# Gate and up products in column halves, their moving operand laid out in DRAM during the attention stage

## The chip, the core and the metric

The kernel runs on one core of a Trainium2 chip. The metric is the device time of one execution in microseconds, as a median over several runs. The core's engines each work through their own instructions in order: TensorE (PE; its weight loads are listed apart as PEld), VectorE (DVE), ScalarE (ACT), GpSimd (POOL) and SyncE (SP). In this kernel SP issues every DMA.

## What is computed

A block of one layer on x of shape (4, 512, 512), all in float32: a layer norm, then attention and a gated feed-forward network side by side, both added to x. The weights of the feed-forward network are not given; they are Catmull-Rom splines through control points.

```python
def spline_reconstruct(control_points, out_size, in_size):
    n = out_size * in_size
    idx, f = _catmull_rom_grid(control_points.shape[0], n)
    p0, p1, p2, p3 = (control_points[idx[0]], ..., control_points[idx[3]])
    w = 0.5 * (2.0 * p1 + (p2 - p0) * f + (2.0 * p0 - 5.0 * p1 + 4.0 * p2 - p3) * f2
               + (3.0 * p1 - p0 - 3.0 * p2 + p3) * f3)
    return w.reshape(out_size, in_size)
...
gate_w = spline_reconstruct(gate_cp, 2048, 512)
up_w = spline_reconstruct(up_cp, 2048, 512)
down_w = spline_reconstruct(down_cp, 512, 2048)
gate = jnp.einsum('bsh,ih->bsi', hidden_states, gate_w)
up = jnp.einsum('bsh,ih->bsi', hidden_states, up_w)
inter = jax.nn.silu(gate) * up
return jnp.einsum('bsi,hi->bsh', inter, down_w)
...
xn = _layernorm(x, axis=-1)
x = x + attention(xn, Wq, bq, Wk, bk, Wv, bv, Wo, bo) + ffn(xn, gate_cp, up_cp, down_cp)
```

A row of gate_w or up_w is a cubic between knots that lie some 129 samples apart. So the kernel doesn't multiply by whole rows of 512 entries. For each of 16 tiles of 128 rows it keeps 64 numbers per token: 44 single samples of xn near the knots (4 windows of 11), and 20 moments, sums of xn against cubics over the stretches between the windows. The product of a tile has a contraction of 64 in place of 512.

## The kernel before

The program has two stages. The **attention stage** covers all four batches: layer norm, projections, scores, softmax, values, and the output projection. It is a loop over 64 units (batch, group of four heads, tile of 128 queries). `items[n]` lists what is added at unit n: a projection, a transpose, a load. In this stage the gate, up and down weights are also built from their control points, by DVE (L600 to L684). `feat[0]`, a tile that stays for the whole program, serves as space for the tables of this work until item 52.

Two things per batch go to DRAM in this stage: the normed x, transposed (`keep_samples`, L491, to `samples[b]`; at items 0, 12, 28 and 44) and the moments (`stretch_moments`, L498, to `moments[b]`; at items 20, 18, 34 and 60). `load_feat` (L525) brings them back as the moving operand `feat[b]`, [128, 2 parts, 4, 512]. Its 128 partitions are four strips of 32 rows, one for each tile of a group of four; a strip holds 22 samples and 10 moments in each part. It issues 24 transfers for a batch, 16 of samples with 11 rows (88 KB) and 8 of moments with 10 rows (80 KB). For batch 0 they stand at item 52; for the others in the second stage.

The **feed-forward stage** follows five written plans (L1201). Plan b does the gate and up products of batch b, and works off the down products of batch b - 1 in between:

- G and U (`gate`, L1075, and `up`, L1080; V is U with other PSUM banks): `product` (L1057) for a group q of four tiles. For each of two parts, each of the four strips is multiplied by its 128 weight columns into its own PSUM bank: 8 matmuls with 32 rows and 128 columns, 512 wide. ACT takes gate's four banks (silu, L1078), DVE multiplies up's four banks by the result (L1085), GpSimd copies it (L1086), and SP moves odd rows between banks (L1090, `inner<-made`) and single rows to `lone` (L1095, L1099).
- m and M (`inner_moments`, L1101): moments of the inner activations, matmuls of 32 rows and 64 columns. The last step is followed by copies and sums on DVE and ACT (T, `add_moments`, L1135).
- R (`down_values`, L1152): the down product from single inner values, matmuls of 32 rows and 64 columns.
- S (`down_moments`, L1172): its part from the moments, 128 rows and 64 columns, then on DVE the addition of attention's result (`res`, loaded by L, L1148) and the store.
- P (`proj`, L466): the rest of batch 3's output projection, 128 rows and 128 columns.
- F: `load_feat` of batch b + 1, in two pieces: F0 with three of the four windows, F1 with the last.

PSUM has two sets of four banks here, `ps_g` for G and U, `ps_o` for V, m, R and P. Every float32 matmul shows as two records in the trace.

The order on each engine is the order of the program (`in_order`, L379, pins it), SP included: an issue that waits holds up all the issues behind it.

Of the kernel before, what the change touches and what calls it, by code (L numbers as in the profile page):

```python
# [12 lines left out]
F32 = mybir.dt.float32  # L13
# [5 lines left out]
P = 128  # L19
B, S, D, H = 4, 512, 512, 16  # L20
# [3 lines left out]
NB = D // P  # L24
# [19 lines left out]
Q32 = 32  # L44
ND = 64
NE = 8
NCV = 5
NX = 9 + 4
NW, NW4 = 11, 4
NST = NW4 + 1  # L50

# [153 lines left out]
def window(g, w):  # L205

    return 8 * g + 129 * w - 1
# [187 lines left out]
def block_kernel(  # L395
# [17 lines left out]
    nc = tc.nc  # L413
    xpf = xp.rearrange("b s d -> (b s) d")

    keep = ctx.enter_context(tc.tile_pool(name="keep", bufs=1))
    dram = ctx.enter_context(tc.tile_pool(name="dram", bufs=1, space=bass.MemoryType.DRAM))
# [7 lines left out]
    samples = [dram.tile([D + P + Q32, S], F32, name=f"samples{b}") for b in range(B)]  # L425
    moments = [dram.tile([NRT * 4 * NST, S], F32, name=f"moments{b}") for b in range(B)]

    feat = {0: keep.tile([P, 2, NB, S], F32, name="feat")}


    wT = keep.tile([P, NB, 4, P], F32, name="wT")
# [90 lines left out]
                if at == k:  # L522
                    nc.sync.dma_start(out=rows[s], in_=o[half * 64 : (half + 1) * 64])

    def load_feat(b, windows=range(NW4)):  # L525

        strip = lambda j: feat[b][j * Q32 : (j + 1) * Q32]
        turns = [(0, 2, 1, 3), (1, 3, 0, 2)]
        for w in windows:
            for j in turns[w % 2]:  # L530
                rows = samples[b][window(j, w) + 1 :][:P].rearrange("(q r) d -> r q d", q=NB)
                nc.sync.dma_start(
                    out=strip(j)[w % 2 * NW : (w % 2 + 1) * NW, w // 2], in_=rows[:NW]
                )
            if w % 2:
                rows = moments[b].rearrange("(q r) d -> r q d", q=NB)
                for j in turns[0]:
                    at = (2 * j + w // 2) * 2 * NST
                    nc.sync.dma_start(
                        out=strip(j)[2 * NW :, w // 2], in_=rows[at : at + 2 * NST]  # L540
                    )


    with ExitStack() as att:
# [19 lines left out]
        for k in range(2):  # L564
# [24 lines left out]
            out=dist[:, S - P :],  # L589
# [10 lines left out]
        def row_weight_steps():  # L600
            size = NB * 2 * P
            shaped = lambda a: a.rearrange("p (q x n) -> p q x n", q=NB, x=2)
            spare = [
                feat[0].rearrange("p h c s -> p (h c s)")[:, k * size : (k + 1) * size]
                for k in range(4)
            ]
            temps = [wd[:, :size], wd[:, size : 2 * size]]
            tabs, points = {}, {}

            def load(c):  # L610
                def go():
                    tabs[c], points[c] = (shaped(a) for a in spare[c % 2 * 2 :][:2])
                    nc.sync.dma_start(out=tabs[c], in_=coef[c])
                    for k in range(NB):
                        strip = slice(k * Q32, (k + 1) * Q32)
                        nc.sync.dma_start(
                            out=spare[c % 2 * 2 + 1][strip],
                            in_=rowpts[c, k].partition_broadcast(Q32),
                        )

                return go

            def term(c, w):
                to = wT[:, :, 2 * w : 2 * w + 2, :]
                tmp = shaped(temps[w]) if c else to

                def times():
                    own = points[c].rearrange("p (w q) x n -> p w (q x) n", w=2)[:, w]
                    own = own.unsqueeze(2).to_broadcast([P, NB, 2, P])
                    nc.vector.tensor_tensor(tmp, tabs[c], own, ALU.mult)  # L630

                def plus():
                    nc.vector.tensor_tensor(to, to, tmp, ALU.add)

                return [times, plus] if c else [times]

            steps = [(0.0, load(0)), (0.0, load(1))]
            for c in range(NCG):
                for w in range(2):
                    steps += [(1.2, half) for half in term(c, w)]  # L640
                if c + 2 < NCG:
                    steps.append((0.0, load(c + 2)))
            return steps


        def down_steps():
            size = 5 * P
            spare = feat[0].rearrange("p h c s -> p (h c s)")
            given, at = [], 0
            for _, lo, hi, _ in DOWN_STEPS:  # L650
                given.append((at, (hi - lo) * P))
                at += P * (hi - lo) * P

            def load(n):
                def go():
                    at, width = given[n]
                    for k, source in enumerate((downtab, downpts)):
                        to = spare[:, (n % 3 * 2 + k) * size :][:, :width]
                        part = source[at : at + P * width].rearrange("(p x) -> p x", p=P)
                        nc.sync.dma_start(out=to, in_=part)  # L660

                return go

            def term(n):
                kind, lo, hi, c = DOWN_STEPS[n]
                width = given[n][1]
                to = (dR if kind == "v" else dM)[:, lo:hi].rearrange("p a n -> p (a n)")
                tmp = wd[:, n % 2 * size :][:, :width] if c else to
                tab, own = (spare[:, (n % 3 * 2 + k) * size :][:, :width] for k in range(2))

                def times():
                    nc.vector.tensor_tensor(tmp, tab, own, ALU.mult)

                def plus():
                    nc.vector.tensor_tensor(to, to, tmp, ALU.add)

                return [times, plus] if c else [times]

            steps = [(0.0, load(n)) for n in range(3)]
            for n in range(len(DOWN_STEPS)):  # L680
                steps += [(0.9, half) for half in term(n)]
                if n + 3 < len(DOWN_STEPS):
                    steps.append((0.0, load(n + 3)))
            return steps  # L684
# [284 lines left out]
        for b in range(B):  # L969
            at = 4 * NHG * b  # L970
            items[max(at - 4, 0)].append(lambda b=b: keep_samples(b))
            items[(20, 18, 34, 60)[b]].append(lambda b=b: stretch_moments(b))
        items[52].append(lambda: load_feat(0))
        weights = deque(row_weight_steps() + down_steps())


# [79 lines left out]

    def product(b, q, w, pool, tag):  # L1057

        ps = [pool.tile([P, S], F32, name=tag) for _ in range(NB)]
        for part in range(2):  # L1060
            for k in range(NB):
                rows = slice(k * Q32, (k + 1) * Q32)
                nc.tensor.matmul(  # L1063
                    ps[k],
                    lhsT=wT[rows, q, 2 * w + part, :],
                    rhs=feat[b][rows, part, q, :],
                    start=(part == 0),
                    stop=(part == 1),
                )
        return ps  # L1070

    around, turning = {}, [False] * B
# [121 lines left out]
    for load, _ in last[:3]:  # L1194
# [4 lines left out]


    plans = [  # L1201
# [5 lines left out]
    ]  # L1207
# [1 line left out]
    def carry_out(b, steps):  # L1209
        for step in steps.split():  # L1210
            kind, which = step[0], step[1:]
            tiles = range(*map(int, which.split(":"))) if ":" in which else None
            if kind == "G":
                gate(b, int(which))
            elif kind == "U":
                up(b, int(which))
            elif kind == "V":
                up(b, int(which), ps_o, "o")
            elif kind == "P":
                last[int(which)][1]()  # L1220
                if int(which) == 0:
                    last[3][0]()
            elif kind == "M":
                inner_moments(b - 1, tiles, ps_g, "g")
            elif kind == "m":
                inner_moments(b - 1, tiles, ps_o, "o")
            elif kind == "F":
                if int(which) == 0:
                    feat[b + 1] = (keep if b % 2 else featp).tile([P, 2, NB, S], F32, name="feat")
                load_feat(b + 1, (range(NW4 - 1), [NW4 - 1])[int(which)])  # L1230
            elif kind == "T":
                add_moments(b - 1, 3)
            elif kind == "R":
                down_values(b - 1, tiles, ps_o, "o")
            elif kind == "L":
                load_res(b - 1)
            else:
                down_moments(b - 1)
# [50 lines left out]
```

## Time and profile before

| | |
|---|---|
| median of 3 runs | 573.04 us (571.2 to 573.11) |
| the profiled execution | 576.39 us |
| its span, first to last instruction | 574.6 us |
| granted TensorE clock, mean | 0.997 |
| first product (L1063) starts | 409.5 us |
| L1063 in `ps_g`, 32x128, 512 wide | 432 records |
| L1063 in `ps_o` | 80 records |
| L1110 (m, M), 32x64 | 512 records |
| L1164 (R), 32x64 | 576 records |
| `feat<-samples` | 64 transfers of 88 KB |
| `feat<-moments` | 32 transfers of 80 KB |
| DMA moved in all | 67.73 MB, 118 GB/s in the mean |

The page gives busy time, the chain of waits that ended last, and groups of instructions by line. The chain, listed in order of time, shows for each step its start, its length and how many records it merges: where one TensorE step follows another without a gap, TensorE set the pace; where a DMA or another engine stands between, that was waited for. The timeline of one engine lists its instructions with the idle time before them. Matmul ends are modelled, so the distance from the start of one step to the start of the next is read, not the busy time. Some matmul records are missing (of L1063's 512 all are there, in two groups).

### The profile page before, as it was taken

The page shows a single profiled execution, that of the slowest core. Times are in us where ns is not written, and L with a number is a line of the kernel's source. Part 1 is how long each engine was busy: PE and PEld are TensorE (multiplying, and loading weights), DVE is VectorE, ACT ScalarE, POOL GpSimd, SP SyncE. Part 2 cuts the span into 40 slices and gives each one's busy share as a digit, 9 for nine tenths or more (in the row PEclk, how much of TensorE's full clock was granted, in tenths as well). Part 3 has the DMA queues.
Part 4 walks back from the last instruction along what each step waited for, and adds up shares of the span by engine and source line. Part 5 has one row for each costly group of instructions (what it writes and reads, how often), then busy time and mean ns, then how long its engine had stood idle before and what let it go on. Part 6 is the DMA issues. An engine that isn't in the chain of part 4 may idle for free.

```text
span 574.6 us, 11201 instructions
## 1 busy us (share of the span) xinstructions
PE 563.5 (98%) x4012; PEld 277.7 (48%) x4012; DVE 355.6 (62%) x990; ACT 295.8 (51%) x782; POOL 184.2 (32%) x332
## 2 busy tenths in 40 slices
PE   7999999999999999999999999999999999999997
PEld 5645555544455555454555555555535334333343
DVE  5169998797587784637544444556243663854747
ACT  2266766565357556554755666677414521613413
POOL 2034534253134343222432442444133223122220
PEclk8999999999999999999999999999999999999999
DMA  8932246326443540212020004603557475685344
GB/s 297 336 83 75 73 116 189 110 50 201 129 156 111 187 164 0 66 38 74 2 88 6 1 2 103 118 6 79 131 134 184 95 191 187 114 196 199 114 150 161
DMA packets 34360, 67.73 MB, mean 118 GB/s; under 512 B 5664, under 2 KB 5664, under 8 KB 33792
## 3 DMA queue, kind: packets, MB, share of 16 engines
q1 hardware_dynamic: 34304, 67.01, 41.2%
q8 instruction: 32, 0.52, 0.4%
q14 instruction: 24, 0.20, 0.1%
HBM read 42.35 MB, written 15.29 MB: 100 GB/s over the span
## 4 chain that ended last, share of the span: by engine, by line
PE 84%; DVE 5%; DMA 5%; ACT 4%; SPq 1%; issue 1%; POOL 0%; DVEq 0%
PE mm L780 18%; PE mm L895 11%; PE mm L811 10%; PE g L1063 7%; PE mm L477 7%; PE s L838 7%; PE c L909 5%; PE o L1164 5%; PE o L1110 3%; PE o L477 3%; ACT p L867 2%; PE o L1181 2%; PE mm L505 2%; DMA inner<-made 2%; PE o L1063 2%; DVE p L851 1%
## 5 line engine op out<-in xcount | busy, mean ns | idle before, releaser
L882 POOL TENSOR_SCALAR p<-p,inv 128x128 f32<-128x128 f32 (+3 forms) x256 | 141.9, 573 | 258.7 <-DVE inv L880 247.1
L867 ACT ACTIVATE p<-p,low 128x128 f32<-128x128 f32 (+3 forms) x256 | 140.7, 552 | 46.3 <-DVE low L851 46.0
L851 DVE CUSTOM_DVE_ANT_0 p<-s,dist 128x128 f32<-128x128 f32 (+3 forms) x256 | 109.2, 482 | 36.7 <-PE s L838 35.7
L895 PEld LDWEIGHTS mm<-ident,p 128*128 128x128 f32 x640 | 71.0, 141 | 40.4 <-issue 25.5
L895 PE MATMUL mm<-ident,p 128*128 128x128 f32 x640 | 89.0, 278 | 1.2 <-ACT pT L900 0.7
L900 ACT COPY pT<-mm 128x512 f32<-128x512 f32 x96 | 55.2, 580 | 53.6 <-PE mm L895 53.3
L1086 POOL COPY made<-inner 128x512 f32<-128x512 f32 x64 | 39.0, 633 | 110.6 <-DVE inner L1085 85.2
L1078 ACT ACTIVATE act<-g 128x512 f32<-128x512 f32 x64 | 33.2, 603 | 63.9 <-PE g L1063 63.9
L811 PE MATMUL mm<-wv,xnT 128*128 128x512 f32 x128 | 59.8, 610 | 2.3 <-ACT xnT L765 2.3
L780 PE MATMUL mm<-xnT,wk 128*128 128x512 f32 (+1 forms) x136 | 59.3, 579 | 0.2 <-ACT xnT L765 0.2
L1063 PE MATMUL g<-feat,wT 32*128 32x512 f32 x432 | 58.6, 611 | 0.0
L780 PE MATMUL mm<-xnT,wq 128*128 128x512 f32 (+1 forms) x136 | 58.0, 569 | 0.3 <-ACT pT L900 0.2
L838 PE MATMUL s<-kT,qT 32*128 32x512 f32 (+3 forms) x512 | 51.1, 468 | 0.3
L898 DVE COPY pT<-mm 128x512 f32<-128x512 f32 x64 | 43.6, 687 | 9.1 <-PE mm L895 8.6
L867 ACT ACTIVATION_READ_ACCUMULATOR p<-p,low 128x1 f32 x256 | 48.4, 189 | 0.0
L1085 DVE TENSOR_TENSOR inner<-g,act 128x512 f32<-128x512 f32 x44 | 27.3, 684 | 31.7 <-issue 20.3
L477 PE MATMUL mm<-ctxT,wo 128*128 128x512 f32 x88 | 40.0, 597 | 0.0
L1063 PEld LDWEIGHTS g<-feat,wT 32*128 32x128 f32 x432 | 23.7, 184 | 32.2 <-issue 20.4
L909 PE MATMUL c<-pT,v 128*32 128x128 f32 (+3 forms) x512 | 37.8, 436 | 0.0
L780 PEld LDWEIGHTS mm<-xnT,wk 128*128 128x128 f32 x136 | 24.5, 189 | 25.3 <-issue 21.9
L811 PEld LDWEIGHTS mm<-wv,xnT 128*128 128x128 f32 x128 | 23.6, 194 | 26.8 <-issue 24.1
L780 PEld LDWEIGHTS mm<-xnT,wq 128*128 128x128 f32 x136 | 24.7, 190 | 23.2 <-issue 22.0
(100 smaller groups left out, 558.2 us busy)
## 6 DMA issues: line engine op xcount, KB each, us to landing
inner<-made SPq DMA_DIRECT2D x32, 256.0 KB
feat<-samples SPq DMA_DIRECT2D x64, 88.0 KB
xp<-in_xp_dram SPq DMA_DIRECT2D x16, 256.0 KB
samples<-xnT SPq DMA_DIRECT2D x4, 1024.0 KB
feat<-in_coef_dram SPq DMA_DIRECT2D x8, 512.0 KB
feat<-in_rowpts_dram SPq DMA_DIRECT2D x32, 128.0 KB
xt<-in_xT_dram SPq DMA_DIRECT2D x16, 256.0 KB
mid<-xt SPq DMA_DIRECT2D x16, 256.0 KB
```

The source lines that it names most:

```text
L477: nc.tensor.matmul(ps, lhsT=wsb["o"][:, c, r * P : (r + 1) * P], rhs=ctxT[b][:, c, :], start=(c == 0), stop=(c == NB - 1),)
L780: nc.tensor.matmul(ps[0][:, tokens], lhsT=wsb[name][:, c, hg * P : (hg + 1) * P], rhs=xnT[b][:, c, tokens], start=(c == 0), stop=(c == NB ...
L811: nc.tensor.matmul(ps[0], lhsT=xnT[b][:, c, t * P : (t + 1) * P], rhs=wsb["v"][:, c, :], start=(c == 0), stop=(c == NB - 1),)
L838: nc.tensor.matmul(banks[b, hg][j][:, at : at + (k + 1) * P], lhsT=qk[b, hg, "q"][rows, k * P : (k + 1) * P], rhs=qk[b, hg, "k"][rows, : ( ...
L851: nc.vector.tensor_tensor_reduce(out=p[:, j, :nk], in0=ps[j], in1=dist[:, S - nk :], scale=-SLOPES[hg * NG + j], scalar=BIG, op0=ALU.add, ...
L867: nc.scalar.activation(p[:, j, :nk], p[:, j, :nk], AF.Exp, bias=low[:, j : j + 1], scale=-1.0, accum_out=total[:, j : j + 1],)
L882: nc.gpsimd.tensor_scalar(p[:, j, :nk], p[:, j, :nk], inv[:, j : j + 1], 1.0, ALU.mult, ALU.mult)
L895: nc.tensor.transpose(ps[:, j, :], p[:, j, c * P : (c + 1) * P], ident)
L898: nc.vector.tensor_copy(out, ps)
L900: nc.scalar.copy(out, ps)
L909: nc.tensor.matmul(ps[j * HD : (j + 1) * HD, c * P :], lhsT=vals[b][:, c, hg * P + j * HD : hg * P + (j + 1) * HD], rhs=w[:, j, :], start= ...
L1063: nc.tensor.matmul(ps[k], lhsT=wT[rows, q, 2 * w + part, :], rhs=feat[b][rows, part, q, :], start=(part == 0), stop=(part == 1),)
```

## The change

`product` cuts the 128 columns of each matmul into two halves of 64, which go to the lower and upper 64 partitions of the same bank: 16 matmuls of 32x64 in place of 8 of 32x128. For each batch there is a new DRAM tensor `table[b]` in the layout of `feat`, which becomes [128, 4, 2, 512]. `lay_out` gives 24 DRAM-to-DRAM transfers for a batch, with the rows and sources of the old loads. They are issued by SP in the attention stage: three in each of items 24 to 31 (batch 0), 32 to 39 (batch 1) and 40 to 47 (batch 2); for batch 3 the 16 of samples at items 56 to 58 and the 8 of moments at 62 to 64. `load_feat(b, q)` is then one transfer of 128 rows with 4 KB each, 512 KB. Batch 0's four stand at item 52; in plans 0 to 2 they are spread out as F0 to F3, each behind an up product.

```diff
+LAID_OUT = [(24, 24), (32, 32), (40, 40), (56, 62)]
...
-    feat = {0: keep.tile([P, 2, NB, S], F32, name="feat")}
+    feat = {0: keep.tile([P, NB, 2, S], F32, name="feat")}
+    table = [dram.tile([P, NB, 2, S], F32, name=f"table{b}") for b in range(B)]
...
-    def load_feat(b, windows=range(NW4)):
-
-        strip = lambda j: feat[b][j * Q32 : (j + 1) * Q32]
-        turns = [(0, 2, 1, 3), (1, 3, 0, 2)]
-        for w in windows:
-            for j in turns[w % 2]:
-                rows = samples[b][window(j, w) + 1 :][:P].rearrange("(q r) d -> r q d", q=NB)
-                nc.sync.dma_start(
-                    out=strip(j)[w % 2 * NW : (w % 2 + 1) * NW, w // 2], in_=rows[:NW]
-                )
-            if w % 2:
-                rows = moments[b].rearrange("(q r) d -> r q d", q=NB)
-                for j in turns[0]:
-                    at = (2 * j + w // 2) * 2 * NST
-                    nc.sync.dma_start(
-                        out=strip(j)[2 * NW :, w // 2], in_=rows[at : at + 2 * NST]
-                    )
+    def lay_out(b, part):
+        for j in range(NB):
+            strip = table[b][j * Q32 : (j + 1) * Q32, :, part]
+            for k in range(2):
+                rows = samples[b][window(j, 2 * part + k) + 1 :][:P].rearrange("(q r) d -> r q d", q=NB)
+                yield strip[k * NW : (k + 1) * NW], rows[:NW]
+            rows = moments[b].rearrange("(q r) d -> r q d", q=NB)
+            yield strip[2 * NW :], rows[(2 * j + part) * 2 * NST :][: 2 * NST]
+
+    def load_feat(b, q):
+        nc.sync.dma_start(out=feat[b][:, q], in_=table[b][:, q])
...
-        items[52].append(lambda: load_feat(0))
+        items[52].extend(lambda q=q: load_feat(0, q) for q in range(NB))
+        for b in range(B):
+            copies = [lay_out(b, part) for part in range(2)]
+            for n, (to, rows) in enumerate(step for part in copies for step in part):
+                at = LAID_OUT[b][n % 3 == 2] + n // (3 if b < 3 else 9)
+                items[at].append(lambda to=to, rows=rows: nc.sync.dma_start(out=to, in_=rows))
...
-                nc.tensor.matmul(
-                    ps[k],
-                    lhsT=wT[rows, q, 2 * w + part, :],
-                    rhs=feat[b][rows, part, q, :],
-                    start=(part == 0),
-                    stop=(part == 1),
-                )
+                for half in range(2):
+                    cols = slice(half * ND, (half + 1) * ND)
+                    nc.tensor.matmul(
+                        ps[k][cols, :],
+                        lhsT=wT[rows, q, 2 * w + part, cols],
+                        rhs=feat[b][rows, q, part, :],
+                        start=(part == 0),
+                        stop=(part == 1),
+                    )
...
-        "F0 G0 P0 U0 F1 P1 G1 P2 U1 P3 G2 V2 G3 V3",
-        "F0 G0 m0:8 U0 L F1 m8:16 G1 T R0:6 U1 T R6:12 G2 R12:16 U2 S G3 V3",
-        "F0 G0 m0:8 U0 L F1 m8:16 G1 T R0:6 U1 T R6:12 G2 R12:16 U2 S G3 V3",
+        "G0 P0 U0 F0 P1 G1 P2 U1 F1 P3 G2 V2 F2 G3 V3 F3",
+        "G0 m0:8 U0 L F0 m8:16 G1 T R0:6 U1 F1 T R6:12 G2 R12:16 U2 F2 S G3 V3 F3",
+        "G0 m0:8 U0 L F0 m8:16 G1 T R0:6 U1 F1 T R6:12 G2 R12:16 U2 F2 S G3 V3 F3",
...
-                    feat[b + 1] = (keep if b % 2 else featp).tile([P, 2, NB, S], F32, name="feat")
-                load_feat(b + 1, (range(NW4 - 1), [NW4 - 1])[int(which)])
+                    feat[b + 1] = (keep if b % 2 else featp).tile([P, NB, 2, S], F32, name="feat")
+                load_feat(b + 1, int(which))
```

More of the change, by code (lines that the diff above doesn't have):

```diff
@@ L603, in row_weight_steps @@
             spare = [
-                feat[0].rearrange("p h c s -> p (h c s)")[:, k * size : (k + 1) * size]
+                feat[0].rearrange("p c h s -> p (c h s)")[:, k * size : (k + 1) * size]
                 for k in range(4)
@@ L647, in down_steps @@
             size = 5 * P
-            spare = feat[0].rearrange("p h c s -> p (h c s)")
+            spare = feat[0].rearrange("p c h s -> p (c h s)")
             given, at = [], 0
```

## The prediction

> **What bounds the kernel now.** First the page: the share of each engine, then the chain of waits.
>
> ```profile
> PE 563.5 (98%) x4012; PEld 277.7 (48%) x4012; DVE 355.6 (62%) x990; ACT 295.8 (51%) x782; POOL 184.2 (32%) x332
> ...
> PE 84%; DVE 5%; DMA 5%; ACT 4%; SPq 1%; issue 1%; POOL 0%; DVEq 0%
> ```
>
> TensorE sets the pace, at a granted clock of 0.997, so a step on it is worth its full length; but the 5% of DMA in the chain says that somewhere TensorE waited on a transfer. Both are read stage by stage. The attention stage ends at 409.5 us, where the first product starts; before it the change alters DMA issues alone. So the chain of waits in order of time, behind it (start, length, engine, tile, line, count):
>
> ```profile
> 527.64 1.93 PE g L1063 x16
> 529.57 2.76 PE o L1164 x48
> 532.33 1.93 PE g L1063 x16
> ...
> 547.22 1.93 PE g L1063 x16
> 549.15 1.72 PE o L1063 x16
> ...
> 447.47 3.62 PE o L1110 x64
> ```
>
> A product (L1063, 8 matmuls, each two records of 32x128) takes 1.93 us after a step of another shape, and 1.72 us when a product went before it. An R step of 48 records of 32x64 takes 2.76, an m step of 64 takes 3.62: 16 records more cost 0.86, so in its own shape R would take 3 x 0.86 = 2.58 and m 4 x 0.86 = 3.44. Each entry into another shape thus costs 0.18 us (R, m) or 0.21 us (products).
>
> Third, the timeline of SP's queue and of TensorE around the end of plan 2 (start, length, engine, line, operation, tiles, count, idle before):
>
> ```profile
> 490.22 3.23 SPq L532 DMA_DIRECT2D feat<-samples  x8
> 493.50 2.77 SPq L539 DMA_DIRECT2D feat<-moments  x4
> 497.62 2.23 SPq L532 DMA_DIRECT2D feat<-samples  x4
> 500.57 1.43 SPq L1090 DMA_DIRECT2D inner<-made  x2
> 502.06 3.11 SPq L1095 DMA_DIRECT2D lone<-made  x4
> 505.21 0.40 SPq L1150 DMA_DIRECT2D res<-mid  x1
> ...
> 508.95 2.00 PE L1063 MATMUL g<-feat,wT 32*128 32x512 f32 x16
> 511.78 3.34 PE L1063 MATMUL o<-feat,wT 32*128 32x512 f32 x15 [0.83 <-DVE res L1190]
> ...
> 511.03 2.49 DVE L1190 TENSOR_TENSOR res<-o,res 128x512 f32<-128x512 f32 x4 [2.94 <-PE g L1063]
> ```
>
> U0 of this plan was multiplied by DVE from 484.44 and copied by GpSimd by 487.6 (485.26 + 2.35), yet its move to the odd rows is issued at 500.57, because the loads of feat stand ahead of it on SP. The load of res behind it goes out at 505.21 instead of some 492, DVE's L1190 starts at 511.03 (5.8 us after that issue; in plan 1 it is 465.51 to 471.57, 6.1 us, and there the wait is named res<-mid; the L1063 named here is no input of L1190), and V3, which takes L1190's banks, waits for it.
>
> **The change part by part.**
>
> 1. *Products in column halves.* 32 products become 16 matmuls of 32x64, with the tile form of R and m: two waves of 16 records, 2 x 0.86 = 1.72 us. The work costs what it did; what goes is the entry between shapes. In plans 1 to 3 the order is G0 m U0 m G1 R U1 R G2 R U2 S: ten entries each, five into m or R (0.18) and five into a product (0.21), 1.95 us. Three plans: -5.85 us. S (128x64) and P (128x128) keep theirs, so plan 0 gains nothing. In plan 4 the entry into M0:12 goes, but M12:16 waits for V3's odd rows (issued 554.23, step at 557.3), so I count 0 there. No row shows a product in 32x64: bounded by nothing gained (1.93) and the wave price (1.72), I take 1.72, since R and m have the same rows, halves, width and one bank per strip.
>
> The cover that shrinks: between U1 and G2 lies only R6:12, then 2.58 us, and DVE empties U1's four banks in 457.88 to 460.36, 2.65 us behind U1's end at 457.71. G2's fourth bank will be some 0.1 late, three times: +0.3. The other pairs have more cover (m8:16 3.44 for DVE's 2.65; R 2.58 for ACT's 2.06).
>
> After the last wave of m8:16, eight halves that end banks, DVE and ACT start at 451.10 and 451.16, against 451.02 where the next step begins; after G1, four such ends, ACT starts at 453.04 against 452.95. So doubling the ends delays a reader by less than 0.05 us, and I take 0. The Trainium skill, "TensorE: Matmul & The Clock Gate", section "The cost: per-tile semaphore tail", adds about 26 ns for each matmul that raises a semaphore, so by it four more ends delay each reader by an estimated 0.1 us, at some twelve places where emptying sets the pace 1.2 us in all, and the forecast would be 563.2. The trace doesn't bear that out.
>
> 2. *Four loads instead of 24.* A plan's 24 issues occupy SP about 11 us (in plan 2, 3.23 + 2.77 + 2.23 before U0's move, 1.89 + 3.60 later); four take about 0.45 each (res and xp loads 0.40 to 0.44), 2 us. They now stand behind the moves of U0, U1, V2/U2 and V3 and behind L, so nothing that TensorE waits for is queued behind F0's issues. Plan 3, which has no F, shows the order without them: res is issued at 532.60, L1190 runs at 546.21 with no wait, and G3 and V3 take 547.15 to 550.80, 3.65 us. A G0 behind them would wait for ACT's last bank (549.17 + 2.06 = 551.23) and take 1.72 + 0.43: 5.80 us from G3 to the m step. Plan 1 takes 470.61 to 478.65 = 8.04, plan 2 508.95 to 518.19 = 9.24. Saved: 2.24 + 3.44. The m8:16 step, clean at 3.62, takes 484.20 to 489.37 = 5.17 in plan 2 (the wait is named inner<-made) and 3.84 in plan 3: 1.55 + 0.22. Together -7.45 us.
>
> Where the stall goes: with V3 early, m0:8's fourth bank comes from DVE's product of V3, which ended 2.72 us behind V3 in plan 3 (551.04 + 2.48 against 550.80), while G0 ends 2.15 behind it: +0.57, at the start of plans 2 and 3: +1.1. Next late would be V3's odd rows: in plan 4 the second half of M waits until 6.5 us behind V3's end, but in plans 2 and 3 that half comes after G0, m0:8, U0 and half of m8:16, 2.7 + 3.4 + 1.7 + 1.7 = 9.5 us: 3 us to spare. G0 needs F0's quarter alone, loaded a plan's length earlier. That a reader waits for its slice and not the whole tile is seen at the start: the first statistics of xp run at 3.47 us, though the fourth slice's load, earlier in the program, had only just been issued. F's bytes stay (2 MB a plan); at the 311 GB/s of the first 20 us, loads of 128 rows, 512 KB take 1.7 us. Contention with the moves: 0 to +1 us, taken 0.
>
> 3. *96 DRAM-to-DRAM transfers in the attention stage.* Three issues in each of items 24 to 47, more around items 56 to 58 and 62 to 64, against 20 fewer at item 52. At 0.45 to 0.6 us (moments<-out: 0.45 to 0.60) three take under 1.8 us of an item's 6.1 (moments of item 18 issued at 129.4, of item 60 at 386.4). SP is idle most of this stretch. Queued behind them: the downtab loads (three sets of buffers, one used up per some 7 us; L672 waited 0.8 us in all), xt loads (issued two items ahead), mid stores, and xp. Samples and moments are written items earlier, so the transfers wait for nothing long. DRAM to DRAM has no row: lower bound 0 (the 20 loads that leave), upper +2 us (four third copies of L520, which wait up to 3.1 us for a landing, each made a little later). Taken 0, since TensorE had under 1 us of waits from 130 to 410 us.
>
> **Sum.** -5.85 + 0.3 - 7.45 + 1.1 = -11.9 us. The profiled execution took 576.39 us (span 574.6 and 1.8 around it): 564.5 after. The three runs have a median of 573.04, 3.35 below the profiled one; some of the waits on landings may be shorter there, so I take 11.0 off: 562.0.
>
> **Rivals.**
>
> - *The halves bring nothing.* The entry may be paid wherever a new input comes in. For: each 1.93 follows such a change. Against: V3 after G3 has a new bank too and takes 1.72. Only part 2: 573.04 - 6.4 = 566.7.
> - *The wait on SP stays.* F0's 512 KB lies in the rings ahead of a move, or V3 waits on L1190 for DVE's own work. For: DMA is 0.6 to 0.75 busy here. Against: plan 3 without F. Only part 1: 573.04 - 5.5 = 567.5.
> - *It doesn't do what it says*: both are given back to the evacuation. DVE is busy 15.8 of 23 us at 489 to 512 and 15.9 of 22 at 530 to 552. If it were the bound, 573.
> - *Slower: the table transfers hold SP.* If an issue waits until the one before has landed (2.5 us, from moments<-out at 386.92 to the copy at 389.4), three of them and 1.2 us of SP's own work make 8.7 us in an item of 6.1. It decides from 1.6 us a transfer on. By item 47 SP is 24 x 2.6 = 62 us behind, makes up some 25 by item 52, and xt for L484 and feat[0] come 35 us late: 573 - 11 + 35 = 597. Against: two moments<-out of interleaved rows of one tensor go out 0.5 us apart, and the 24 loads at 350 to 365 us took 0.6 us each.
>
> **How the numbers follow.** Forecast 0.60, halves bring nothing 0.10, SP's wait stays 0.12, no change 0.09, slower 0.09. Faster is 0.82, the same 0.09, slower 0.09, with 0.5% (2.9 us) as what can be told from no change. The range runs from the forecast with a few more waits gone, 557, to the two one-sided rivals with part 3's 2 us on top, 569.5; no change and slower are left out.
>
> **What would show it.** Products at 1.72 us beside m and R, R at 2.58, m at 3.44; res issued within 6 us of U0 and no idle time before V3; G3 to m0:8 in about 5.8 us in plans 1 and 2; the first product still near 409.5 us. Wrong if products stay at 1.93, if SP still issues inner<-made 5 us or more behind GpSimd's copy, if G0 waits for a load of feat, or if the first product comes over 2 us later.

## The result and the profile after

The new kernel takes 564.2 us in the median of 4 runs (562.7 to 565.48), the old one 573.08 beside it (571.2 to 576.6): a ratio of 0.9845, 95% interval 0.9807 to 0.9883. The forecast was 562.0 in a range of 557.0 to 569.5. The profiled execution took 565.48 us with a span of 563.4 at a mean granted clock of 0.997, against 576.39, 574.6 and 0.997.

First the page of the new kernel, its line of engine shares and the chain's shares by engine:

```profile
PE 553.7 (98%) x4524; PEld 297.0 (53%) x4524; DVE 355.4 (63%) x990; ACT 295.4 (52%) x782; POOL 184.3 (33%) x332
...
PE 86%; DVE 6%; ACT 4%; DMA 3%; issue 1%; SPq 0%; DVEq 0%
```

512 matmul records more, and TensorE is busy 10 us less. The share of DMA in the chain fell from 5% to 3%. The chain in order of time, in plan 2 (start, length, engine, tile, line, records):

```profile
484.72 1.29 PE g L1070 x24
486.43 2.15 PE o L1171 x40
489.01 1.29 PE g L1070 x24
490.73 2.15 PE o L1171 x40
493.30 1.29 PE g L1070 x24
```

The steps now overlap at their borders, so a few records of each are listed apart; the distance from start to start is read. A product (L1070) takes 1.71 and 1.72 us, an R step (L1171) 2.58 and 2.57, as forecast. SP's queue and DVE's L1197 (the old L1190) in the same plan:

```profile
484.81 1.36 SPq L1097 DMA_DIRECT2D inner<-made  x2
486.22 2.85 SPq L1102 DMA_DIRECT2D lone<-made  x4
489.12 0.40 SPq L1157 DMA_DIRECT2D res<-mid  x1
489.62 1.14 SPq L540 DMA_DIRECT2D feat<-table  x1
...
501.10 2.53 DVE L1197 TENSOR_TENSOR res<-o,res 128x512 f32<-128x512 f32 x4
```

The load of res goes out at 489.12, in the old kernel at 505.21; counted from the start of G3 in the plan before, that is 19.6 us in place of 34.6. L1197 starts with no idle time before it.

The best summary of a profile here is the distance between the starts of G3 in successive plans, since each holds one full plan's work. From the timelines of TensorE (the columns are the stretches; the first is the attention stage up to the first product, the last runs from G3 of plan 3 to the end):

| profiled execution | start to first product | to G3 of plan 0 | to plan 1 | to plan 2 | to plan 3 | to the end |
|---|---|---|---|---|---|---|
| old | 409.53 | 25.77 | 35.31 | 38.34 | 38.20 | 27.45 |
| new | 410.42 | 25.62 | 33.49 | 33.29 | 33.24 | 27.34 |
| difference | +0.89 | -0.15 | -1.82 | -5.05 | -4.96 | -0.11 |

The differences add up to -11.2 us, the change of the span.

### The profile page after: what moved, and what is told of

Same layout as the page of the kernel before. It is cut to its first block, busy times and chain, and to the rows that moved or that the text cites. A ratio compares the mean times of both kernels' runs of the same rounds, so it can differ in the third digit from the quotient of the medians.

```text
span 563.4 us, 12222 instructions
## 1 busy us (share of the span) xinstructions
PE 553.7 (98%) x4524; PEld 297.0 (53%) x4524; DVE 355.4 (63%) x990; ACT 295.4 (52%) x782; POOL 184.3 (33%) x332
## 4 chain that ended last, share of the span: by engine, by line
PE 86%; DVE 6%; ACT 4%; DMA 3%; issue 1%; SPq 0%; DVEq 0%
PE mm L779 17%; PE mm L894 11%; PE mm L810 9%; PE g L1070 9%; PE mm L480 7%; PE s L837 6%; PE o L1171 6%; PE c L908 5%; PE o L1117 4%; PE o L1188 3%; PE o L480 3%; ACT p L866 2%; PE mm L508 2%; DVE p L850 2%; PE o L1070 2%; PE g L1117 1%
## 5 line engine op out<-in xcount | busy, mean ns | idle before, releaser
L1070 PE MATMUL g<-feat,wT 32*64 32x512 f32 x864 | 66.7, 592 | 0.0
L1070 PEld LDWEIGHTS g<-feat,wT 32*64 32x64 f32 x864 | 32.4, 131 | 20.0 <-issue 8.6
L1171 PE MATMUL o<-inner,dRM 32*64 32x512 f32 x512 | 38.2, 588 | 0.0
```

Source lines behind the costliest of these rows:

```text
L1070: nc.tensor.matmul(ps[k][cols, :], lhsT=wT[rows, q, 2 * w + part, cols], rhs=feat[b][rows, q, part, :], start=(part == 0), stop=(part == 1),)
L1171: nc.tensor.matmul(sums[b][r][cols, :], lhsT=dR[rows, a, cols], rhs=o[rows, :], start=(a == 0), stop=False,)
```

## The experiments

Each kernel was timed beside the old one; its ratio to the old one is given with a 95% interval. The old kernel scatters: its medians in these comparisons are 571.38 (31 runs), 571.52 (19) and 573.07 us (17), single runs 569.02 to 577.03. The new kernel, measured again with 6 runs, took 563.35 us, 562.55 to 565.54, ratio 0.9842 (0.9802 to 0.9882).

> The new kernel unchanged, for a comparison with the next three on one chip. All theories: near 563.5 us, with little scatter.

### One part at a time

The halves alone, in the old kernel:

```diff
-                nc.tensor.matmul(ps[k], lhsT=wT[rows, q, 2 * w + part, :], rhs=feat[b][rows, part, q, :], ...)
+                for half in range(2):
+                    cols = slice(half * ND, (half + 1) * ND)
+                    nc.tensor.matmul(ps[k][cols, :], lhsT=wT[rows, q, 2 * w + part, cols], rhs=feat[b][rows, part, q, :], ...)
```

> The old kernel with the products in column halves; feat is still loaded by 24 transfers. Theory A (the two parts add up, as the prediction had it): 30 entries between shapes go, -5.5 us against the old kernel, span near 569. Theory B (SP's queue, which issued without a pause from 451 us to the end of plan 2, sets the time of V3's and m8:16's ends in plans 1 and 2): what TensorE saves there is waited for again; only the seven entries behind m8:16 of plan 3 count, 7 x 0.195 = 1.4 us, so -1.5 us, span near 573.

569.81 us, ratio 0.9972 (0.9948 to 0.9995): 1.6 us faster, as theory B has it. The profile says where the rest went. G3 to G3 is 33.49 us into plan 1, as in the new kernel, but then 37.84 and 36.58. SP's queue and DVE in plan 2:

```profile
500.26 0.41 SPq L1152 DMA_DIRECT2D res<-mid  x1
...
506.19 2.48 DVE L1192 TENSOR_TENSOR res<-o,res 128x512 f32<-128x512 f32 x4 [3.21 <-PE g L1065]
```

DVE waits 3.21 us, until 5.9 us after the issue of res (the product L1065 named in the brackets is no input of L1192; res is). From one issue of res to the next (462.18 to 500.26) it is 38.1 us, whatever TensorE has saved. The 36.58 us into plan 3 are not all SP's: behind a wait of 0.77 us for the banks that L1192 empties, TensorE was granted half its clock (0.50) for some 3.4 us, which costs about 1.7 us (length; busy time of TensorE, its weight loads, DVE, ACT and GpSimd, each with its count; granted clock; DMA share; GB/s):

```profile
509.00:513.00 4.00, 4.00 (x50) 2.58 (x42) 2.48 (x4) 0.00 (x0) 1.85 (x4) 0.57 0.88 211
```

Into plan 2 (37.84 us) the clock was 1.00.

The loads alone, in the new kernel: the diff above taken back.

> The new kernel with the products in 128 columns again. A and B alike: the waits of 7.45 us go, 1.1 us of a new wait and 1.0 us in the attention stage come in, -5.4 us against the old kernel, span near 569.2. The steps keep 1.93, 2.76 and 3.62 us. If the halves also relieve something that the loads need, the gain is under 4 us.

568.66 us, ratio 0.9958 (0.9938 to 0.9978): 2.4 us faster by the ratio, 2.7 between the medians (571.38 beside it). Its plans take 35.30, 35.14 and 35.08 us: the waits are gone and what is left is TensorE's own work in the old shape. From the first product to the end it takes 158.7 us, 6.37 less than the old kernel's profile (165.07), where the prediction had 6.35. That the timed gain is smaller than 5.4 lies, as far as the medians tell, in the old kernel: its profiled execution was 3 to 5 us above its medians. Not all of that is waits, since its clock was 0.91 in the first 20 us (last section). The next run, with the old second stage, has plans of 36.18 and 37.49 us in its profile.

So the parts don't add up: -0.3% and -0.4% alone, -1.55% together.

### What the tables cost

The old kernel with the table transfers added, unread:

```diff
         items[52].append(lambda: load_feat(0))
+        for b in range(B):
+            copies = [lay_out(b, part) for part in range(2)]
+            for n, (to, rows) in enumerate(step for part in copies for step in part):
+                at = LAID_OUT[b][n % 3 == 2] + n // (3 if b < 3 else 9)
+                items[at].append(lambda to=to, rows=rows: nc.sync.dma_start(out=to, in_=rows))
```

> The old kernel with the 96 DRAM-to-DRAM transfers issued as in the new one; nobody reads the tables, feat is loaded the old way. If these transfers cost the attention stage its 0.96 us: the first product starts near 410.4 us in place of 409.5, DVE waits 2 to 3 us for a table of the down weights near 205 us, and the whole is 0.6 to 1.0 us slower. If the 0.96 us came from somewhere else: 409.5 us and no such wait.

573.52 us, ratio 1.0042 (1.0009 to 1.0075): 2.4 us slower, more than the 0.6 to 1.0 expected, with an interval of 0.5 to 4.3 us that reaches down to it. The first product's start doesn't tell it, as it differs between executions from the first microseconds on (last section). But the distances between the values steps (L909) do: the one from 190 to 214 us is 24.35 us in the old kernel, 25.30 here, and 24.7 to 25.6 in the profiles of six other kernels with early tables, the new one (24.99) among them; in the second profile of the new kernel it is 24.35. DVE's waits in the attention stage, here:

```profile
DVE wd L685 <- DMA feat<-in_downpts_dram: 2.7, 1, 2.7
```

One wait of 2.7 us for a table of the down weights (0.8 in the old kernel), behind the table transfers on SP. Over the profiles the stretch grows with this wait: 24.34 or 24.35 us where it is 1.5 us or less, 24.74 at 2.1, 24.99 at 2.4, 25.30 at 2.7, 25.56 at 2.9. A second loss of 0.27 us, from 337 to 361 us, shows in all kernels with tables, in the next ones too; its cause stays open.

The new kernel with the transfers put off, `LAID_OUT = [(33, 33), (41, 41), (49, 49), (57, 62)]`, run twice:

> The new kernel with the table transfers of batches 0 to 2 put off to items 33, 41 and 49 on, behind the building of the weights, and batch 3's samples at 57. If the transfers cost by standing ahead of the down weights' tables near 205 us: DVE no longer waits there, the first product starts 0.6 to 0.9 us earlier (409.6 to 409.9 us), the whole is 0.6 to 0.9 us faster than the new kernel. If it is their load on the DMA engines anywhere: no change.

> The new kernel with the table transfers put off behind the building of the weights, once more beside the new kernel. If they cost 0.6 to 0.8 us by standing ahead of the down weights' tables: that much faster than the new kernel in the same runs. If the earlier difference came from the chip: equal.

561.69 us, ratio 0.9833 (0.981 to 0.9857), and 562.77, ratio 0.9829 (0.979 to 0.9869) beside 563.35 for the new kernel. The stretch is 24.34 us in both profiles, with waits of 0.4 and 0.5 us, so the cause is right. The gain of 0.6 us between the medians is inside the scatter (561.83 to 564.52 against 562.55 to 565.54), so a faster kernel isn't shown; the profiles give back some 0.3 us in plan 1 (33.8 us from G3 to G3 against 33.49).

### Place or count of the loads

All 24 loads of a batch behind U0's moves and L, in the old kernel:

```diff
-        "F0 G0 m0:8 U0 L F1 m8:16 G1 T ...",
+        "G0 m0:8 U0 L F0 F1 m8:16 G1 T ...",
```

> The old kernel with all 24 loads of a batch behind U0's moves and L in plans 1 and 2; count, size and all else as before. If it is the place of the loads ahead of res and of U0's moves (A): L1190 no longer waits for res, the 5.7 us from G3 to m0:8 go, -4 to -5 us. If it is SP's whole issue time in a plan, some 35 us and landings (B): another wait takes their place, 0 to -1 us.

573.49 us, ratio 1.0042 (1.0012 to 1.0071). Not faster. Res is in time now, but the plans still take 37.85 and 37.14 us. TensorE in plan 2, where G0 needs its own feat and M's second half V3's moved rows:

```profile
471.22 2.06 PE L1063 MATMUL g<-feat,wT 32*128 32x512 f32 x10
473.68 1.82 PE L1063 MATMUL g<-feat,wT 32*128 32x512 f32 x6 [0.40 <-DMA feat<-moments]
...
480.97 1.97 PE L1110 MATMUL o<-inner,basist 32*64 32x512 f32 x32
483.46 2.56 PE L1110 MATMUL o<-inner,basist 32*64 32x512 f32 x32 [0.52 <-DMA inner<-made]
485.95 2.00 PE L1063 MATMUL g<-feat,wT 32*128 32x512 f32 x16
```

From G0 to m0:8 it is 4.20 us (471.22 to 475.42), against 2.50 in the kernel with the loads alone: the loads, issued later, come late for G0. The step of M takes 4.98 us in place of 3.62. So other waits took the place of the one removed. The issues of res are 39.0 us apart (451.94 and 490.94).

The new kernel with each load cut into six, and into three:

```diff
-        nc.sync.dma_start(out=feat[b][:, q], in_=table[b][:, q])
+        for j in range(NB):
+            rows = slice(j * Q32, (j + 1) * Q32)
+            for parts in (slice(0, 1), slice(1, 2)) if j < 2 else (slice(0, 2),):
+                nc.sync.dma_start(out=feat[b][rows, q, parts], in_=table[b][rows, q, parts])
...
+        for rows in (slice(0, Q32), slice(Q32, ND), slice(ND, P)):
+            nc.sync.dma_start(out=feat[b][rows, q], in_=table[b][rows, q])
```

> The new kernel with each load of feat cut into 6 transfers by strip and part, 24 for a batch, in the same places; bytes and tables as in the new one. If SP's issue time in a plan binds (B): some 11 us of issues come back, SP's queue is full again for 31 us and landings of a plan of 33.3, +2 to +5 us against the new kernel. If it was the place alone (A), or the bytes: 0 to +1 us.

> The new kernel with each load of feat cut in 3 transfers, 12 for a batch in place of 4 (24 cost all of the gain). If a plan takes the longer of TensorE's and SP's time: 8 more issues of 0.6 us put SP at some 27 us and landings of a plan of 33.3, so nothing is lost, 0 to +0.7 us. If each issue costs its own time: 16 issues more in the two plans, +4 us or more; by the split in 6, half of its loss.

Six: 573.35 us, ratio 1.0033 (1.001 to 1.0057), the whole gain lost, some 10 us where B expected 2 to 5. Three: 563.49 us, ratio 0.9845 (0.9789 to 0.9901), nothing lost, plans of 33.49, 33.30 and 33.24 us. So there is a limit between 12 and 24, and below it an issue costs nothing. SP in the six-piece kernel, behind U1's moves in plan 1, and TensorE where it waits in plan 2:

```profile
468.93 3.80 SPq L543 DMA_DIRECT2D feat<-table  x6
...
475.60 4.20 SPq L543 DMA_DIRECT2D feat<-table  x6
479.90 2.13 SPq L1201 DMA_DIRECT2D out_dram<-res  x4
482.12 1.45 SPq L1100 DMA_DIRECT2D inner<-made  x2
...
485.17 4.46 PE L1120 MATMUL o<-inner,basist 32*64 32x512 f32 x32 [2.99 <-DMA inner<-made]
```

Six loads take SP 3.8 and 4.2 us, V3's moves go out at 482.12, and M's second half waits 2.99 us. That wait costs twice its length, as the windows show:

```profile
482.00:485.00 3.00, 0.18 (x2) 0.00 (x0) 0.32 (x1) 0.00 (x0) 1.00 (x2) 0.99 1.03 383
485.00:489.00 4.00, 3.83 (x33) 1.66 (x41) 0.00 (x0) 0.00 (x0) 0.00 (x0) 0.50 0.16 45
489.00:492.00 3.00, 3.00 (x40) 1.14 (x32) 2.28 (x4) 1.56 (x3) 0.00 (x0) 0.54 0.47 118
```

After 3 us without work TensorE was granted half its clock from 485 to about 492 us: some 3 us more. That plan took 40.49 us.

How full SP's queue is can be added up from its single records, from one issue of res to the next in plans 1 and 2: the issues, and the waits that are put down to the landing of an earlier transfer. The time between is given beside them; what is left is other waits and idle time.

| kernel | loads in a plan | issues | landing waits | from res to res |
|---|---|---|---|---|
| new | 4 | 21.1 | 2.8 | 32.0 |
| new, each load in three | 12 | 26.9 | 3.5 | 33.1 |
| new, each load in six | 24 | 32.0 | 2.5 | 38.0 |
| old | 24 | 26.8 | 9.8 | 39.7 |
| old with halves | 24 | 26.8 | 7.8 | 38.1 |
| old, loads behind L | 24 | 27.0 | 8.8 | 39.0 |

In the old kernel the two largest of the landing waits are these (in total, times, longest):

```profile
SPq L539 <- DMA res<-mid: 2.4, 1, 2.4
SPq L532 <- DMA feat<-samples: 2.4, 4, 1.3
```

TensorE's own work in a plan is 33.3 us, or 35.1 in the old shape. The old loads' issues alone, 27 us, would fit into that; with the landing waits they do not.

The four loads at the start of a plan, in the new kernel:

```diff
...
-        "G0 m0:8 U0 L F0 m8:16 G1 T R0:6 U1 F1 T R6:12 G2 R12:16 U2 F2 S G3 V3 F3",
+        "F0 F1 F2 F3 G0 m0:8 U0 L m8:16 G1 T R0:6 U1 T R6:12 G2 R12:16 U2 S G3 V3",
...
```

> The new kernel with the four loads of a batch all at the start of plans 0 to 2, ahead of G0, U0's moves and L. With 0.45 to 0.6 us each on SP they put U0's moves off by 2.4 us, and nothing waits for those that soon: within 0.5 us of the new kernel. If it is the load's bytes in the rings ahead of moves and res, 2 MB at once at some 300 GB/s = 7 us: V3 waits for res or m8:16 for the moves again, +2 to +5 us.

563.02 us, ratio 0.9851 (0.9823 to 0.9878), plans of 33.48, 33.30 and 33.29 us: the place of four loads is worth nothing, and 2 MB at once delayed nothing that shows in the plans.

### The loads on another queue

Halves, the 24 small loads, no tables, and GpSimd issues them for batches 1 to 3:

```diff
+        queue = nc.gpsimd if b else nc.sync
-                nc.sync.dma_start(
+                queue.dma_start(
...
-        "F0 G0 m0:8 U0 L F1 m8:16 G1 T R0:6 U1 T ...",
+        "G0 m0:8 U0 L F0 m8:16 G1 T R0:6 U1 F1 T ...",
```

> The old kernel with column halves and its 24 small loads of a batch from samples and moments, no tables; but for batches 1 to 3 GpSimd issues them, in two pieces behind U0 and behind U1. If SP's issue time was what bound plans 1 and 2, and neither the count nor the size of the transfers matters: G3 to G3 in 33.3 us as in the new kernel, and without the tables' cost in the attention stage 0.5 to 1 us faster than the new kernel. If the small transfers themselves hold up the DMA engines, or GpSimd's issues its copies: above 35 us, and 4 us or more slower than the new kernel.

575.67 us, ratio 1.0054 (1.0021 to 1.0087): 12.3 us slower than the new kernel, with plans of 39.88, 38.70 and 36.71 us. The expectation's first branch failed and its second, that GpSimd's issues hold up its copies, came. GpSimd's timeline in plan 1:

```profile
465.99 2.17 POOL L533 DMA_DIRECT2D feat<-samples  x4
470.82 0.55 POOL L533 DMA_DIRECT2D feat<-samples  x1 [2.66 <-DMA feat<-moments]
473.34 1.62 POOL L533 DMA_DIRECT2D feat<-samples  x3 [1.97 <-DMA feat<-moments]
474.95 0.55 POOL L540 DMA_DIRECT2D feat<-moments  x1
...
479.05 0.55 POOL L540 DMA_DIRECT2D feat<-moments  x1 [0.78 <-DMA feat<-samples]
479.59 4.49 POOL L1089 COPY made<-inner 128x512 f32<-128x512 f32 x8
```

An issue takes 0.55 us, but after the first nine of the plan eight of the other fifteen wait for the landing of an earlier one, 0.2 to 2.7 us each: the second twelve hold GpSimd from 465.99 to 479.6, and the copies of U2 and V3 stand behind them. The next G0 also waits for feat (3.3 us at most). SP had some 19 us of issues in the plan and sent res at 459.48, so it was no longer late. The clock has a part in the loss: behind three of TensorE's pauses (3.15, 3.28 and 1.40 us) it was 0.50 for 3.4 to 6.8 us, which can account for some 6.8 of the 15.4 us by which this profile exceeds the new kernel's from the first product on (168.37 against 152.98).

### The shape itself, or the entry into it

Only gate in halves, in the new kernel:

```diff
-                for half in range(2):
-                    cols = slice(half * ND, (half + 1) * ND)
+                for half in range(2 - w):
+                    cols = slice(half * ND, (half + 1) * ND) if w == 0 else slice(0, P)
```

> The new kernel with halves in the gate products only; up has 128 columns again. If the cost is the entry into another shape: G behind m or R keeps 1.72 us, U behind m or R takes 1.93, R and m behind U 2.76 and 3.62, R behind G 2.58; six entries come back in each of plans 1 to 3, 3 x 1.2 = +3.6 us against the new kernel, span near 567. If products in halves are cheaper by themselves, whatever stands before them: half of the gain of 5.6 goes, +2.8 us, and R and m behind U stay at 2.58 and 3.43.

568.3 us, ratio 0.996 (0.9941 to 0.9978). TensorE in plan 2:

```profile
484.89 1.92 PE L1070 MATMUL g<-feat,wT 32*64 32x512 f32 x32
486.61 2.96 PE L1171 MATMUL o<-inner,dRM 32*64 32x512 f32 x48
489.50 2.00 PE L1070 MATMUL g<-feat,wT 32*128 32x512 f32 x16
491.43 2.83 PE L1171 MATMUL o<-inner,dRM 32*64 32x512 f32 x48
494.05 2.09 PE L1070 MATMUL g<-feat,wT 32*64 32x512 f32 x32
495.77 2.09 PE L1171 MATMUL o<-inner,dRM 32*64 32x512 f32 x32
```

From start to start, R before a product of its own shape takes 2.62 us (491.43 to 494.05), R before one of 128 columns 2.89; U before R takes 1.93, G before R 1.72. The cost lies at the border between shapes, on the step that is left. With half the products in halves, only 0.35 of the 5.72 us between the profiles of the loads alone (158.70 us from the first product on) and the new kernel (152.98) is kept (158.35): the product in halves is no cheaper, the border is what cost. I had counted six borders that come back and +3.6; there are seven (V3 behind G3 too), and more in plan 0's G2 V2 G3 V3, and it is +5.4 in the profiles, 1.53 to 1.58 a plan, or 0.22 a border.

## Why the prediction was right, point by point

- *Entries between shapes, -5.85 and +0.3 for G2.* Right in the sum and in the mechanism of the entries, which the gate run shows. Into plan 1, where nothing else changes, -1.85 was due (1.95 less 0.1) and -1.82 came. G2 itself was not late, though: in plan 2 it takes 1.72 us (492.32 to 494.04), as a clean product does. About 0.1 us a plan is missing elsewhere, the profile doesn't show where, so that the 0.3 fits is luck.
- *Waits behind SP, -7.45, and the new wait for V3's fourth bank, +1.1.* Right in size for the profiled execution: -1.85 - 2.24 - 1.55 + 0.57 = -5.07 to plan 2, and -5.05 came; -1.85 - 3.44 - 0.22 + 0.57 = -4.94 to plan 3, and -4.96 came. The reason given, that issues stand ahead of res and of the moves, was only half of it. Putting them elsewhere didn't help, 12 in place of 4 cost nothing, 24 cost everything: SP's queue, with its waits for landings, takes 36 to 40 us for a plan with 24 loads, and a plan takes the longer of that and TensorE's own time. The 11 us that the prediction gave to the 24 issues mixes two things: the rows that it names add up to 13.7 us, and the single issues in them to 8.2 (0.27 to 0.36 us each); the rest is waits for landings.
- *The tables, taken as 0, bounds 0 and +2.* Mis-sized: +0.89 in the profiles, 0.6 of it from a wait for the down weights' tables that I had called covered. The issue was priced at 0.45 to 0.6 us; DRAM to DRAM takes SP 0.72 to 0.81 as a rule.
- *From the profile to the median.* 11.0 was taken off the median, 8.9 came. The old kernel's profiled execution was 3.3 us above its median, the new one's 1.3 above its own, and both began at a clock of 0.91. That leaves some 2 us which the old kernel lost in this execution and not in its median one; that they are waits of SP's queue, which vary from run to run, is likely but not shown. The allowance for all of it, 0.9 us, was too small.
- *The rivals.* Single parts were priced at 566.7 and 567.5 as if they added up; measured alone they give 568.66 and 569.81, which is 2.7 and 1.6 us under the old kernel beside them (571.38) where 6.4 and 5.5 were priced. For the halves the miss is of kind: while SP sets the pace, a faster TensorE waits for it. Transfers that hold SP in the attention stage did not come: the new kernel's tables are issued in 2.3 to 2.8 us a set of three, where that rival had 8.7.
- *Semaphore tail.* By the Trainium skill, "TensorE: Matmul & The Clock Gate", section "The cost: per-tile semaphore tail", the sum would have been an estimated 563.2. The plans came out within 0.03 us of the sum without it, so the trace doesn't show it here.

## What to carry to other kernels

Where an in-order queue issues all DMAs, add up its issues and landing waits over one period of the loop and set them beside the busiest engine's time: the period is the longer of the two, so a saving on either shows only while it is the longer one, and two changes can be worth more together than apart. Neighbouring matmul steps in one tile shape save the border between shapes, even with twice the instructions. A wait that disappears should be traced to what is late next, before its whole length is booked as a gain.

## What was not expected of the hardware

- Pauses on TensorE were followed by half the granted clock (0.50) for some 3.4 or 6.7 us: one of 2.99 us with the six-piece loads, ones of 3.15, 3.28 and 1.40 us with GpSimd's issues, and one of only 0.77 us in the old kernel with halves. Other pauses as short as that one, of 0.71 and 0.83 us in the old kernel and 0.77 in plan 1 of the six-piece kernel, showed no drop (1.00). So the length of a pause alone doesn't decide it, and the cause stays open.
- In the first 20 us the granted clock was 0.91 in four profiles (the old and the new kernel's first ones among them), and the first values step then began at 58.4 to 59.4 us; in the ten others it was 1.00 and 56.4 to 57.3 us. Spans of single profiles differ by 2 us from that alone, so stretches were compared, not spans.
- A DRAM-to-DRAM transfer of 80 or 88 KB kept SP's queue for 0.72 to 0.81 us as a rule, a load of 512 KB in 128 rows for 0.40 to 0.58 (1.14 and 1.29 once each), an old load of 80 or 88 KB for 0.27 to 0.36.
